# Narrower treatment of the entering steps in a windowed scan of test-time updates

## The chip, the cores and the metric

The kernel runs on one core of a Trainium2 chip. The metric is device time in microseconds (us), the median of several runs; before the change it is 901.47 us (three runs, 900.8 to 902.53). A profiled execution gives the trace that is read below. The engines are TensorE (PE for its matmuls, PEld for its weight loads), VectorE (DVE), ScalarE (ACT), GpSimd (POOL) and SyncE (SP), which here only issues transfers.

## The reference

Two layers follow one another on an input of 4 sequences, 1024 steps and 128 features. The second is a mixture of experts (8 experts, the best two of them for each token, and one shared expert); the change doesn't touch it. The first is a small two-layer network whose weights are trained while the sequence is read:

```python
def loss_fn(params, k_t, v_t):
    return jnp.mean((_mlp(params, k_t) - v_t) ** 2)

def step(params, kvt):
    k_t, v_t = kvt
    g = jax.grad(loss_fn)(params, k_t, v_t)
    new_params = tuple((p - LR * gp for p, gp in zip(params, g)))
    return (new_params, None)
params, _ = jax.lax.scan(step, (W1, b1, W2, b2), (k, v))
q = x @ W_Q
return _mlp(params, q)
```

Each of the 1024 steps sees 4 columns of k and v, one for each sequence, computes the gradient with the weights that all earlier steps have left, and takes one step of gradient descent. Only the weights after the last step are used further.

## The kernel before

The scan isn't run step by step. A window of `WIN = 32` steps, that is `R = 128` columns, slides over the sequence and advances by 6 and 7 steps in turn (`ADV = 7`). In each pass of the loop at line 555 (162 passes) all steps of the window are computed at once, from the weights as they stand before the window and from corrections for the steps of the window that lie earlier. The corrections use the previous pass's results, so that a step's values are refined about five times while it crosses the window. When steps leave at the front of the window, their update goes into the weights for good.

The main names are these:

- `z` (line 489): the hidden layer's input from the weights (`base`), to which line 569 adds the correction `dz` times `gm`. `gm` holds masked products of keys. They are computed in bands of 128 rows (`multiply` and `masked`, lines 382 to 403), written to DRAM (`g_dram`) and loaded again for each pass by `load_products` (line 319), six passes ahead, on SP's queue. Fourteen bands are computed before the scan, the others two at a time in the first passes.
- `at` and `th` (lines 598 and 600): Silu and tanh of `z`, on ACT; `mT` (line 607) combines them on DVE for the derivative.
- `y` (lines 582 and 613): the network's output; `nm` is the masked product of activations (`pg`, half 0, line 622), and `er` the errors of the previous pass.
- `et` (line 636): errors, `y` minus the wanted values; `vb` (`values`, line 494) are those values with the bias.
- `da` (lines 632 and 648): the gradient at the hidden layer; `hm` (line 579) is the masked product of errors (`pg`, half 1, line 659).
- `dz` (line 655): the gradient at the hidden layer's input.
- lines 678 and 679: POOL copies the leaving rows of `dz` and `er` (`dl`, `el`), with which `pu` and `pv` (lines 508 and 516) update the weights in the next pass.
- `add_changes` (line 533): POOL sums the squared changes of values between passes in `ch`, `sq`, `va` and `sums`. After the scan these sums decide whether the scan has converged. If it hasn't, a plain loop over all 1024 steps is run (line 730).

A window column exists only for the 32 steps inside. But the loop works ahead: `AHD = 7` steps next to enter, `AHD * B = 28` columns, are carried beside the 128 of the window, so the tiles are `C = R + 28 = 156` columns wide. For these, z, its correction, the activation, y with its correction, and the error are computed too. The products of activations and errors for the next pass (lines 622 and 659) then have columns for all steps of the next window.

The scan is under a manual schedule: each engine's instructions stand in the order in which the program writes them. On TensorE a pass has the order z from the correction, y from `nm`, `pu`, `pv`, y from the activations, the transposition of `at`, products of activations, transposition of `u`, transposition of `mT`, the two parts of `da`, transposition of `et`, products of errors, z of the next pass from the weights, transposition of `v`. Products of 32-bit numbers are two instructions each on TensorE, transpositions one. Each PSUM tile of the scan has one buffer.

Of the kernel before, what the change touches and what calls it, by code (L numbers as in the profile page):

```python
# [10 lines left out]
F32 = mybir.dt.float32  # L11
AF = mybir.ActivationFunctionType
ALU = mybir.AluOpType
# [4 lines left out]
P = 128  # L18
# [7 lines left out]
def kernel(  # L26
# [23 lines left out]
    nc = tc.nc  # L50
    B, S, D = x.shape
# [14 lines left out]
    AHD = ADV  # L66
    R = WIN * B
    Q = ADV * B
    C = R + AHD * B
# [9 lines left out]
    const = ctx.enter_context(tc.tile_pool(name="const", bufs=1))  # L79
# [49 lines left out]
    ident = const.tile([P, P], F32, name="ident")  # L129
# [13 lines left out]
    before = const.tile([P, WIN + ADV, B], F32, name="before")  # L143
# [24 lines left out]


    ad_bufs = [const.tile([P, D + 1], F32, name=f"ad{i}") for i in range(2)]  # L170
    nm_bufs = [const.tile([P, C], F32, name=f"nm{i}") for i in range(2)]
    dl_bufs = [const.tile([P, D], F32, name=f"dl{i}") for i in range(2)]
    el_bufs = [const.tile([P, D], F32, name=f"el{i}") for i in range(2)]

# [4 lines left out]
    def constants(n):  # L179

        if n == 0:


            nc.gpsimd.memset(before, -ALPHA)
            nc.gpsimd.affine_select(
                out=before, in_=before, compare_op=ALU.is_gt, fill=0.0, base=0,
                pattern=[[B, WIN + ADV], [0, B]], channel_multiplier=-1,
            )
        elif n == 1:
            for i in range(2):  # L190
                for t in (nm_bufs[i], dl_bufs[i], el_bufs[i]):
                    nc.gpsimd.memset(t, 0.0)
            nc.gpsimd.memset(sums, 0.0)
            nc.gpsimd.dma_start(eb1[:, 0:NE, :], e_b1)
            nc.gpsimd.dma_start(eb1[:, NE, :], s_b1)
        elif n == 2:
            nc.gpsimd.memset(eb1r, 0.0)
            nc.gpsimd.dma_start(wr_sb, w_router_t)
            nc.gpsimd.dma_start(sw1, s_w1t)
            nc.gpsimd.dma_start(sw2, s_w2t)  # L200
        elif n == 3:
            nc.gpsimd.memset(eb2, 0.0)
            for i in range(BLK):
                r = i * (P // BLK)
                nc.gpsimd.dma_start(eb2[r:r + NE, i, :], e_b2)
                nc.gpsimd.dma_start(eb2[r + NE:r + NX, i, :], s_b2.rearrange("(o d) -> o d", o=1))
        elif n == 4:
            sort_c["lane"] = iota("lane", [P], [[1, P]])
            sort_c["part"] = iota("part", [1], [[0, 1]], mult=1)
            sort_c["row1"] = iota(  # L210
                "row1", [TOP_K, NT], [[1, TOP_K], [TOP_K * P, NT]], base=1, mult=TOP_K
            )
            sort_c["edge"] = iota("edge", [NT], [[P, NT]])
            nc.gpsimd.memset(tri, 1.0)
            nc.gpsimd.affine_select(
                out=tri, in_=tri, compare_op=ALU.is_gt, fill=0.0, base=0, pattern=[[1, P]],
                channel_multiplier=-1,
            )
            for i in range(2):
                nc.gpsimd.memset(cum[i][:, 0:NT // 2, :], 0.0)  # L220
                nc.gpsimd.memset(ends[i][:, 0:NE // 2], 0.0)
# [41 lines left out]
    with tc.tile_pool(name="scanbig", bufs=1) as sbig, tc.tile_pool(  # L263
        name="kdram", bufs=1, space=DRAM
# [8 lines left out]
        g_dram = kdp.tile([NR, NR], F32, name="g_dram")  # L273
# [17 lines left out]
        PF = 6  # L291
# [27 lines left out]
        def load_products(i, queue):  # L319


            (op, pe), (o, e) = span(i - 1), span(i)
            el = min(e + AHD, S)
            gm = sp_.tile([P, C], F32, name="gm", bufs=PF + 1)
            queue.dma_start(
                gm[0:(pe - op) * B, 0:(el - o) * B], g_dram[op * B:pe * B, o * B:el * B]
            )
            return gm

# [45 lines left out]
            nc.sync.dma_start(tok(k_tok, j), kr)  # L375


        GW = Q + C + P
        gw_bufs = [sp_.tile([P, P + GW], F32, name=f"gw{i}", bufs=1) for i in range(4)]
        flat = before.rearrange("p s b -> p (s b)")  # L380

# [56 lines left out]
        for n in range(NBLK + 1):  # L438
# [19 lines left out]
            if n > B:  # L458
                for _ in range(4):
                    if todo[0] < early:  # L460
                        pg = bank("pgk", "k", [GW], 4)
# [6 lines left out]
            if n == B + 2:  # L468
                load_keys(0, nc.gpsimd)
                gms = {i: load_products(i, nc.gpsimd) for i in range(1, PF + 1)}  # L470
        load_keys(1, nc.gpsimd)
        front.close()
        before = flat
# [10 lines left out]
        with tc.tile_pool(name="s_ps", bufs=1, space=PSUM) as sps, tc.manual_schedule():  # L484
# [9 lines left out]
            def values(i, v):  # L494

                o, e = span(i)
                n = (min(e + AHD, S) - o) * B
                vb = sp_.tile([P, C], F32, name="vb")
                nc.scalar.activation(  # L499
                    vb[:, 0:n], vc[:, o * B:o * B + n], AF.Identity, bias=v[:, D:D + 1],  # L500
                    scale=-1.0,
                )
                return vb
# [44 lines left out]
            wa, wc, u, v = a_bufs[0], c_bufs[0], u_bufs[0], v_bufs[0]  # L548
# [3 lines left out]
            z = base(0, wa, True)  # L552
            vb = values(0, v)
            prev = pg = None
            for i in range(NI):
                o, e = span(i)
                op, pe = span(i - 1) if i else (0, 0)
                on, en = span(i + 1)
                ro, rn, q, qn = (pe - op) * B, (e - o) * B, (o - op) * B, (on - o) * B
                rc, nx = (min(e + AHD, S) - o) * B, (en - on) * B  # L560
# [1 line left out]

                y = sps.tile([P, C + P], F32, name="y")
                da = sps.tile([P, D], F32, name="da")
                if prev:
                    ae_p, ad_p, er_p, dz_p, q_p = prev
                    nc.tensor.matmul(  # L569
                        z[:, 0:rc], lhsT=dz_p[0:ro, :], rhs=gms.pop(i)[0:ro, 0:rc],  # L570
                        start=False, stop=True,
                    )
                    nm = nm_bufs[i % 2]
                    nc.vector.scalar_tensor_tensor(  # L574
                        nm[0:ro, 0:rn], pg[0:ro, 0, 0:rn], 1.0, before[0:ro, q:q + rn],
                        ALU.add, ALU.mult,
                    )
                    hm = sp_.tile([P, R], F32, name="hm")
                    nc.vector.tensor_tensor(
                        hm[0:ro, 0:rn], pg[0:ro, 1, 0:rn], before[0:ro, q:q + rn], ALU.mult  # L580
                    )
                    nc.tensor.matmul(  # L582
                        y[:, 0:rc], lhsT=er_p[0:ro, :], rhs=nm[0:ro, 0:rc],
                        start=True, stop=False,
                    )
                if i + PF < NI and i:
# [10 lines left out]
                at, et = ae[:, 0, :], ae[:, 1, :]  # L597
# [5 lines left out]
                if more is not None:  # L603
# [7 lines left out]


                nc.tensor.matmul(  # L613
                    y[:, 0:rc], lhsT=wc, rhs=at[:, 0:rc], start=not prev, stop=True
                )
                ta = z[:, C:C + P]
                nc.tensor.transpose(ta[0:rn, :], at[:, 0:rn], ident)  # L617
# [2 lines left out]
                if not last:  # L620
                    pg = sps.tile([P, 2, R], F32, name="pg")
                    nc.tensor.matmul(
                        pg[0:rn, 0, 0:nx], lhsT=at[:, 0:rn], rhs=at[:, qn:qn + nx],
                        start=True, stop=True,
# [6 lines left out]
                if prev:  # L631
                    nc.tensor.matmul(  # L632
                        da[0:rn, :], lhsT=hm[0:ro, 0:rn], rhs=ad_p[0:ro, 0:D],
                        start=True, stop=False,
                    )
                nc.vector.tensor_tensor(et[:, 0:rc], y[:, 0:rc], vb[:, 0:rc], ALU.add)
                v_new = update(v_bufs, v, pv) if q else v

                if not last:
                    vb = values(i + 1, v_new)  # L640
# [7 lines left out]
                nc.tensor.matmul(  # L648
                    da[0:rn, :], lhsT=et[:, 0:rn], rhs=v[:, 0:D], start=not prev, stop=True
                )  # L650
                nc.tensor.transpose(y[0:rn, C:C + P], et[:, 0:rn], ident)
                er = sp_.tile([P, D], F32, name="er")
                nc.scalar.copy(er[0:rn, :], y[0:rn, C:C + P])
                dz = sp_.tile([P, D], F32, name="dz")
                nc.vector.scalar_tensor_tensor(  # L655
                    dz[0:rn, :], da[0:rn, :], 0.5, dr[0:rn, :], ALU.mult, ALU.mult
                )
                if not last:
                    nc.tensor.matmul(
                        pg[0:rn, 1, 0:nx], lhsT=et[:, 0:rn], rhs=et[:, qn:qn + nx],  # L660
                        start=True, stop=True,
                    )
                    z = base(i + 1, wa, False)
                if q:
                    turn(pv, v_new)
                    wc = turned(c_bufs, wc, pv)
# [9 lines left out]
                if qn:  # L676
                    dl, el = dl_bufs[i % 2], el_bufs[i % 2]
# [7 lines left out]
                prev = (ae, ad, er, dz, q)  # L685
# [8 lines left out]
            wa, wc = turned(a_bufs, wa, pu), turned(c_bufs, wc, pv)  # L694
# [3 lines left out]
        with tc.tile_pool(name="f_sb", bufs=1) as fp, tc.tile_pool(  # L698
            name="f_ps", bufs=1, space=PSUM
# [30 lines left out]
        with tc.If(again > 0):  # L730
            load_params(wa, wc, u, v, nc.scalar)
            half_bias(u)
            with tc.tile_pool(name="o_sb", bufs=1) as op_, tc.tile_pool(
                name="o_ps", bufs=1, space=PSUM
            ) as ops:
                with tc.For_i(0, S, 1) as t:
# [22 lines left out]
                    for k, src in enumerate((kt, a1, d1, e1)):  # L759
# [19 lines left out]
                        start=True, stop=True,  # L779
# [13 lines left out]
    with ExitStack() as stage, tc.tile_pool(  # L793
        name="e_pa", bufs=3, space=PSUM
    ) as pa, tc.tile_pool(name="e_py", bufs=2, space=PSUM) as epy, tc.tile_pool(
        name="e_pt", bufs=2, space=PSUM
# [159 lines left out]
        at, d = 0, 1  # L956
        while d < NT:
# [3 lines left out]
            at, d = 1 - at, 2 * d  # L961
# [19 lines left out]
        at, d = 0, 1  # L981
        while d < NE:
# [4 lines left out]
            at, d = 1 - at, 2 * d  # L987
# [42 lines left out]
        for n, (k, g) in enumerate(groups):  # L1030
# [15 lines left out]
            for i in range(GC):  # L1046
                nc.tensor.matmul(  # L1047
                    inv, lhsT=sel[:, i, :], rhs=val[:, i, :],
                    start=(n == 0 and i == 0), stop=(n == len(groups) - 1 and i == GC - 1),
# [74 lines left out]
        for t in range(3):  # L1124
# [5 lines left out]
            rhs=code.rearrange("p t f -> p (t f)"), start=True, stop=True,  # L1130
# [4 lines left out]
        for h in range(2):  # L1135
            pg = bank(ept, "pg", "t", [NBLK // 2, P])
# [10 lines left out]
        prev = None  # L1147
        for t in range(NTL):
# [10 lines left out]
            prev = (t, hs, ws.pop(t)[1])  # L1159
# [77 lines left out]
```

## Time and profile before

| | |
|---|---|
| median of three runs | 901.47 us |
| profiled execution | 901.75 us |
| its span, first to last instruction | 899.9 us |
| mean granted TensorE clock | 0.974 of full speed |
| PE busy / PEld busy | 811.0 us (90%) / 741.6 us (82%) |
| DVE busy / ACT busy / POOL busy | 525.2 / 503.8 / 554.2 us |
| scan with its first passes | about 65 to 575 us |
| y from nm (line 582), 128x156 | mean 330 ns of one instruction, 196 between 200 and 500 us |
| y from the activations (line 613), 128x156 | mean 311 ns |
| z from gm (line 569), 128x156 | mean 298 ns |
| products of errors (line 659), 128x128 | mean 275 ns |
| values (line 499), 128x156 | mean 424 ns |
| errors (line 636), 128x156 | mean 321 ns |

[...] What one costs in a stream is the distance from its start to the start of the next matmul, which the view in order of time shows. In that view "x2" means two instructions merged in one row, with the time from the start of the first to the end of the second. Times in the trace are counted from the start of the span.

### The profile page before, as it was taken

What the parts mean: (1) busy time and instruction counts of PE and PEld (TensorE: products, weight loads), DVE (VectorE), ACT (ScalarE), POOL (GpSimd) and SP (SyncE); (2) the same over time, 40 slices, a digit from 0 to 9 for tenths busy, and PEclk for the clock granted to TensorE, in tenths of its full rate; (3) what the DMA queues carried; (4) which work ended last, traced back from release to release, by engine and by line L of the source; (5) the groups of instructions that cost most, each with busy time, mean ns of one, the idle gap of its engine ahead of it and who ended that gap; (6) DMA issues with size and microseconds to landing.
All of it is one profiled execution on the core that took longest, in us unless ns stands there. A gap on an engine that the chain in (4) does not pass through costs nothing. (4 is left out here: it accounts for less than half of the span.)

```text
span 899.9 us, 21051 instructions
## 1 busy us (share of the span) xinstructions
PE 811.0 (90%) x6164; PEld 741.6 (82%) x6164; DVE 525.2 (58%) x1904; ACT 503.8 (56%) x1571; POOL 554.2 (62%) x1513
## 2 busy tenths in 40 slices
PE   4789999999999999999999999788999999999830
PEld 3456899999999999999999999555479999899730
DVE  5634577677677677767767776475973232223227
ACT  2564566666666666666666666355623444444432
POOL 6630577777777777777777777521015777777730
PEclk9999999999999999999999999998999999999975
DMA  5273311121111111121111110002115777778755
GB/s 129 73 233 119 97 31 27 26 49 27 28 29 39 34 30 26 29 46 27 29 28 26 30 27 7 2 25 71 58 42 163 243 254 237 240 241 259 248 172 167
DMA packets 77892, 82.48 MB, mean 92 GB/s; under 512 B 9907, under 2 KB 57023, under 8 KB 77777
## 3 DMA queue, kind: packets, MB, share of 16 engines
q1 hardware_dynamic: 68880, 68.16, 25.2%
q0 software_dynamic: 5632, 10.07, 4.1%
q10 hardware_dynamic: 3264, 2.89, 1.0%
q8 instruction: 51, 0.84, 0.4%
q14 instruction: 65, 0.52, 0.2%
HBM read 64.03 MB, written 17.97 MB: 91 GB/s over the span
## 5 line engine op out<-in xcount | busy, mean ns | idle before, releaser
L1097 ACT ACTIVATE hs<-ph,b1t 128x128 f32<-128x128 f32 x284 | 81.1, 369 | 109.2 <-PE ph L1093 100.8
L678 POOL COPY dl<-dz 24x128 f32<-24x128 f32 (+2 forms) x158 | 44.5, 281 | 148.9 <-DVE dz L655 148.9
L1066 POOL DMA_INDIRECT xg<-h_tab,toks_i x71 | 72.9, 1026 | 73.8 <-DVE toks_i L1062 52.4
L521 DVE SCALAR_TENSOR_TENSOR u<-pu,u 128x130 f32<-128x130 f32 x158 | 46.4, 294 | 115.3 <-PE pu L508 115.3
L546 POOL TENSOR_TENSOR sums<-sums,sq 128x48 f32<-128x48 f32 (+2 forms) x315 | 93.8, 317 | 0.0
L1110 POOL DMA_INDIRECT y_tab<-yg,rows_i x71 | 72.5, 1021 | 29.7 <-issue 13.1
L619 ACT COPY ad<-z 128x128 f32<-128x128 f32 (+3 forms) x162 | 43.0, 265 | 73.0 <-PE z L617 73.0
L582 PE MATMUL y<-nm,er 128*128 128x156 f32 (+4 forms) x322 | 79.3, 328 | 3.1 <-DVE nm L574 2.7
L1093 PE MATMUL ph<-xT,w1t 128*128 128x128 f32 x568 | 75.3, 276 | 0.7 <-DVE xT L1086 0.7
L1105 PE MATMUL py<-w2t,hs 128*128 128x128 f32 x568 | 74.9, 275 | 0.0
L613 PE MATMUL y<-ae,c 128*128 128x156 f32 (+3 forms) x324 | 73.2, 307 | 0.0
L530 ACT COPY c<-pv 128x128 f32<-128x128 f32 x158 | 42.0, 266 | 52.5 <-PE pv L526 49.6
L569 PE MATMUL z<-gm,dz 128*128 128x156 f32 (+4 forms) x322 | 69.7, 298 | 0.2
L1093 PEld LDWEIGHTS ph<-xT,w1t 128*128 128x128 f32 x568 | 68.9, 191 | 0.9 <-DVE xT L1086 0.9
L489 PE MATMUL z<-kT,a 128*128 128x156 f32 (+3 forms) x324 | 69.6, 296 | 0.0
L1105 PEld LDWEIGHTS py<-w2t,hs 128*128 128x128 f32 x568 | 69.0, 192 | 0.0
L499 ACT ACTIVATE vb<-vT,v 128x156 f32<-128x156 f32 (+3 forms) x162 | 68.2, 421 | 1.4 <-DVE dr L642 1.0
L539 POOL TENSOR_TENSOR sq<-ch 128x104 f32<-128x104 f32 (+1 forms) x158 | 56.9, 360 | 12.4
L598 ACT ACTIVATE ae<-z,u 128x156 f32<-128x156 f32 (+3 forms) x162 | 62.8, 387 | 2.8 <-PE z L569 0.9
L648 PE MATMUL da<-v,ae 128*128 128x128 f32 (+3 forms) x324 | 62.9, 276 | 0.1
L632 PE MATMUL da<-ad,hm 128*128 128x128 f32 (+3 forms) x322 | 62.4, 275 | 0.0
L538 POOL TENSOR_TENSOR ch<-ae 128x104 f32<-128x104 f32 (+1 forms) x158 | 62.4, 395 | 0.0
(245 smaller groups left out, 2390.9 us busy)
## 6 DMA issues: line engine op xcount, KB each, us to landing
w1t<-in_e_w1t_dram SPq DMA_DIRECT2D x71, 256.0 KB
w2t<-in_e_w2t_dram SPq DMA_DIRECT2D x71, 256.0 KB
gm<-g_dram SPq DMA_DIRECT2D x150, 78.0 KB
g_dram<-gw SPq DMA_DIRECT2D x29, 220.0 KB
x_sb<-in_x_dram SPq DMA_DIRECT2D x8, 256.0 KB
k_dram<-kr SPq DMA_DIRECT2D x8, 256.0 KB
h_tab<-hr SPq DMA_DIRECT2D x8, 256.0 KB
hs_all<-y_tab ACTq DMA_DIRECT2D x4, 512.0 KB
```

What stands on the lines that cost most here:

```text
L489: nc.tensor.matmul(z[:, 0:n], lhsT=wa, rhs=kc[:, o * B:o * B + n], start=True, stop=alone)
L499: nc.scalar.activation(vb[:, 0:n], vc[:, o * B:o * B + n], AF.Identity, bias=v[:, D:D + 1], scale=-1.0,)
L546: nc.gpsimd.tensor_tensor(t, t, x_[:, :, c0:c1], ALU.add)
L569: nc.tensor.matmul(z[:, 0:rc], lhsT=dz_p[0:ro, :], rhs=gms.pop(i)[0:ro, 0:rc], start=False, stop=True,)
L582: nc.tensor.matmul(y[:, 0:rc], lhsT=er_p[0:ro, :], rhs=nm[0:ro, 0:rc], start=True, stop=False,)
L613: nc.tensor.matmul(y[:, 0:rc], lhsT=wc, rhs=at[:, 0:rc], start=not prev, stop=True)
L648: nc.tensor.matmul(da[0:rn, :], lhsT=et[:, 0:rn], rhs=v[:, 0:D], start=not prev, stop=True)
L1066: nc.gpsimd.indirect_dma_start(out=xg_bufs[t % 6][:], out_offset=None, in_=h_tab[:, :], in_offset=bass.IndirectOffsetOnAxis(ap=toks_i[:, t ...
L1093: nc.tensor.matmul(ph[:, f, :], lhsT=w1t[:, ts(f, P)], rhs=xT, start=True, stop=True)
L1097: nc.scalar.activation(hs[:, f, :], ph[:, f, :], AF.Gelu_apprx_tanh, bias=b1t[:, t, f:f + 1])
L1105: nc.tensor.matmul(py, lhsT=hs[:, f, :], rhs=w2t[:, f, :], start=(f == 0), stop=(f == NFC - 1))
L1110: w = nc.gpsimd.indirect_dma_start(out=y_tab[:, :], out_offset=bass.IndirectOffsetOnAxis(ap=rows_i[:, t:t + 1], axis=0), in_=yg[:], in_off ...
```

## The change

For the steps next to enter, only z from the weights (without its correction) and the activation from it are still computed. The correction of z, both parts of y, the values, the errors and the products of errors have columns for the window alone. The steps that have just entered therefore have no products of errors from the previous pass: these columns of `hm` are zero. `hm` moves to two fixed buffers that are zeroed once, and only its first `ro - q` columns are written in each pass; where a pass writes fewer columns than the pass before it in the same buffer, a memset clears the rest. `nm` moves to the rotating pool in exchange. The key products lose the 28 columns in their bands (`GW`) and in `gm`.

```diff
-    nm_bufs = [const.tile([P, C], F32, name=f"nm{i}") for i in range(2)]
+    hm_bufs = [const.tile([P, R], F32, name=f"hm{i}") for i in range(2)]
...
-            el = min(e + AHD, S)
-            gm = sp_.tile([P, C], F32, name="gm", bufs=PF + 1)
+            gm = sp_.tile([P, R], F32, name="gm", bufs=PF + 1)
             queue.dma_start(
-                gm[0:(pe - op) * B, 0:(el - o) * B], g_dram[op * B:pe * B, o * B:el * B]
+                gm[0:(pe - op) * B, 0:(e - o) * B], g_dram[op * B:pe * B, o * B:e * B]
             )
...
-        GW = Q + C + P
+        GW = Q + R + P
...
-                n = (min(e + AHD, S) - o) * B
-                vb = sp_.tile([P, C], F32, name="vb")
+                n = (e - o) * B
+                vb = sp_.tile([P, R], F32, name="vb")
...
-                y = sps.tile([P, C + P], F32, name="y")
+                y = sps.tile([P, R + P], F32, name="y")
...
-                        z[:, 0:rc], lhsT=dz_p[0:ro, :], rhs=gms.pop(i)[0:ro, 0:rc],
+                        z[:, 0:rn], lhsT=dz_p[0:ro, :], rhs=gms.pop(i)[0:ro, 0:rn],
                         start=False, stop=True,
                     )
-                    nm = nm_bufs[i % 2]
+                    nm = sp_.tile([P, R], F32, name="nm")
...
-                    hm = sp_.tile([P, R], F32, name="hm")
+                    hm = hm_bufs[i % 2]
                     nc.vector.tensor_tensor(
-                        hm[0:ro, 0:rn], pg[0:ro, 1, 0:rn], before[0:ro, q:q + rn], ALU.mult
+                        hm[0:ro, 0:ro - q], pg[0:ro, 1, 0:ro - q], before[0:ro, q:ro],
+                        ALU.mult,
                     )
+                    if hm_cols[i % 2] > ro - q:
+                        nc.vector.memset(hm[:, ro - q:hm_cols[i % 2]], 0.0)
+                    hm_cols[i % 2] = ro - q
                     nc.tensor.matmul(
-                        y[:, 0:rc], lhsT=er_p[0:ro, :], rhs=nm[0:ro, 0:rc],
+                        y[:, 0:rn], lhsT=er_p[0:ro, :], rhs=nm[0:ro, 0:rn],
...
-                    y[:, 0:rc], lhsT=wc, rhs=at[:, 0:rc], start=not prev, stop=True
+                    y[:, 0:rn], lhsT=wc, rhs=at[:, 0:rn], start=not prev, stop=True
...
-                nc.vector.tensor_tensor(et[:, 0:rc], y[:, 0:rc], vb[:, 0:rc], ALU.add)
+                nc.vector.tensor_tensor(et[:, 0:rn], y[:, 0:rn], vb[:, 0:rn], ALU.add)
...
-                        pg[0:rn, 1, 0:nx], lhsT=et[:, 0:rn], rhs=et[:, qn:qn + nx],
+                        pg[0:rn, 1, 0:rn - qn], lhsT=et[:, 0:rn], rhs=et[:, qn:rn],
```

Here `o` and `e` are the first step and the end of the window, `rn` its columns, `rc` those with the steps ahead, `ro` the columns of the previous window, and `q` the columns by which the window has advanced.

More of the change, by code (lines that the diff above doesn't have):

```diff
@@ L190, in constants @@
             for i in range(2):
-                for t in (nm_bufs[i], dl_bufs[i], el_bufs[i]):
+                for t in (hm_bufs[i], dl_bufs[i], el_bufs[i]):
                     nc.gpsimd.memset(t, 0.0)
@@ L554 @@
             prev = pg = None
+            hm_cols = [0, 0]
             for i in range(NI):
@@ L650 @@
                 )
-                nc.tensor.transpose(y[0:rn, C:C + P], et[:, 0:rn], ident)
+                nc.tensor.transpose(y[0:rn, R:R + P], et[:, 0:rn], ident)
                 er = sp_.tile([P, D], F32, name="er")
-                nc.scalar.copy(er[0:rn, :], y[0:rn, C:C + P])
+                nc.scalar.copy(er[0:rn, :], y[0:rn, R:R + P])
                 dz = sp_.tile([P, D], F32, name="dz")
```

## The prediction

> **What bounds the kernel now.** I read the views from coarse to fine. The busy tenths by slice put TensorE at 9 in every slice from about 70 us to 560 us: that stretch is the scan, the only part that the diff touches apart from one band width before it. The busy time by stretch shows what fills it:
>
> ```profile
> 200.00:250.00 50.00, 50.00 (x412) 49.38 (x410) 34.92 (x132) 33.84 (x116) 37.57 (x132) 1.00 0.11 28
> ```
>
> The columns after the length are PE, PEld, DVE, ACT and POOL busy, then the granted clock (1.00), the DMA share and GB/s. PE and PEld are full, but matmul ends are modelled, so "full" alone doesn't say that a shorter matmul makes a shorter pass. For that I took the scan's period apart in the order of time, from the start of one `da<-v,ae` (D) to the next. A steady pass (columns: start us, us, engine, line, operation):
>
> ```profile
> 404.54 0.39 PE L648 MATMUL da<-v,ae 128*128 128x128 f32 x2
> ...
> 406.33 0.36 POOL L539 TENSOR_TENSOR sq<-ch 128x104 f32<-128x104 f32 x1
> 406.44 0.30 PEld L613 LDWEIGHTS y<-ae,c 128*128 128x128 f32 x2
> ...
> 406.70 0.37 DVE L607 SCALAR_TENSOR_TENSOR mT<-ae,th 128x128 f32<-128x128 f32 x1
> 406.81 0.27 PE L617 MATMUL z<-ident,ae 128*128 128x128 f32 x1
> ...
> 407.58 0.39 PE L648 MATMUL da<-v,ae 128*128 128x128 f32 x2
> ```
>
> The period is 407.58 - 404.54 = 3.04 us. There are 147 of them: the group of mT between 106 and 556 us has 147 entries, and 147 x 3.05 = 448 us.
>
> The most useful rows stand at the end of the scan. Where the sequence runs out, the extra columns vanish by themselves, and one pass of the old kernel already runs z, y and the values 128 wide:
>
> ```profile
> 557.52 0.39 PE L648 MATMUL da<-v,ae 128*128 128x128 f32 x2
> ...
> 559.32 0.36 POOL L539 TENSOR_TENSOR sq<-ch 128x104 f32<-128x104 f32 x1
> 559.36 0.30 PEld L613 LDWEIGHTS y<-ae,c 128*128 128x128 f32 x2
> ...
> 559.65 0.41 DVE L607 SCALAR_TENSOR_TENSOR mT<-ae,th 128x128 f32<-128x128 f32 x1
> 559.68 0.27 PE L617 MATMUL z<-ident,ae 128*128 128x128 f32 x1
> ...
> 560.51 0.39 PE L648 MATMUL da<-v,ae 128*128 128x128 f32 x2
> ```
>
> Its period is 2.99 us. The reader is to see three things. The transposition at line 617 comes at D + 2.27 in the steady pass and at D + 2.16 here, so TensorE did gain 0.11 us. The square on POOL ends at the same place in both (D + 2.15 and D + 2.16). And mT, the next DVE operation, runs from there: 406.70 is 0.01 behind the end of sq at 406.69, and although the 128-wide pass records mT from 559.65, it takes 0.41 instead of 0.37, and ends at D + 2.54 against D + 2.53. So half of TensorE's gain was lost again, waiting for mT.
>
> **The change part by part.** Widths become 128 instead of 156 in three matmuls of two passes each (z from gm, y from nm, y from wc), in the values (ACT), in the errors (DVE), and in the gm transfer; 100 or 104 instead of 128 in the key products of the errors (line 659) and hm; 284 instead of 312 in the band products (line 384). Nothing is moved: no instruction changes its place on an engine, and no wait is added in the scan. The base matmul (line 489) and Silu stay 156 wide.
>
> *TensorE.* In the steady pass a 156-wide matmul starts its successor 0.27 us later (405.47 to 405.74, z from gm), a 128-wide one 0.22 (404.54 to 404.76). So z from gm, y from nm and y from wc should give 3 x 0.05 = 0.15. The last products with 104 columns gave 0.20 against 0.22 (560.84 to 561.04), 0.02 more: 0.17 in all if TensorE alone set the pace. [...] PEld is busy 49.38 of 50 us. [...]
>
> *What the gain runs into.* I follow the chain in the new kernel from D, with durations from the two passes. dz starts at D + 0.48 and ends at 0.77, unchanged. The load for z from gm follows 0.05 behind dz (405.31 to 405.36; 558.30 to 558.35), so the 0.02 of the products brings nothing. Its second pass starts two loads later (0.215), ends 0.275 after that, and Silu follows 0.10 later: D + 1.41 (it was 1.46; 1.42 at the end of the scan). Silu takes 0.39, and the load for y from wc comes 0.05 behind: 1.85. The transposition follows 0.32 later instead of 0.37: 2.17. By TensorE's order alone the next da would stand 0.77 later, as in the steady pass (406.81 to 407.58): D + 2.94, a gain of 0.10.
>
> But tm needs mT. mT reads two SBUF tensors while POOL reads SBUF. [...] sq hangs on dz through POOL's queue (dl, el, ch, sq), and none of these change; so sq ends at D + 2.15, mT at 2.53. From the end of mT to da the 128-wide pass took 0.45 (560.06 to 560.51), as did a pass near the start (89.23 to 89.68). New period: 2.98, a gain of **0.06**. [...] I take 0.06, since the end of the scan is the nearest row there is.
>
> 147 x 0.06 = **8.8 us**.
>
> *The first passes* also multiply a band each time. Sixteen of these are 312 wide inside the scan, 0.53 us apart in the stretch at 92.31 to 92.84, and lose 28 columns: 28/312 x 0.53 = 0.05 each, 0.8 us, on the path since masking, nm and u wait for them (0.41 us idle before y from nm there). The narrower y in the last four of these passes gives 2 x 0.05 x 4 = 0.4. Together **1.2 us**. Before the scan 14 bands lose 0.05 each, but only some lie on TensorE's path between other stages: 0 to 0.7, I take **0.5**.
>
> *Costed at nothing.* The values (424 ns at 156, 0.40 at 128) end well before y needs them. hm is behind nm, and ahead of u, which waits 69.8 us over 98 passes (0.71 each) for its matmul. The errors shrink from 0.32 to 0.28, but wait for mT. gm shrinks from 78 to 64 KB on SP's queue, asked for six passes ahead, and no engine waits for it. Three memsets of hm in the last passes (24 and 52 columns), at most 0.16 us each by the smallest mT, also lie in front of u. If the cover were gone they would cost 0.5 us. [...]
>
> **Sum**: 8.8 + 1.2 + 0.5 = 10.5 us. Against the profiled execution, 901.75 us (span 899.9), 891.2. That run lies 0.28 above the median shown, 901.47; so 891.0.
>
> **The rivals.** [...] (2) *TensorE alone*: 0.17 x 147 + 1.7 = 26.7, **875 us**. For it, two full rows; against it, the loads behind dz, Silu and mT all come within 0.06 of the ends that they wait for. (3) *Weight loads or the POOL chain hold everything*: gain under 0.02 a pass, 898 to **901 us**. The tail's 2.99 speaks against it, but that is one pass. [...] (5) *The change isn't what it says*: the scan tests its own convergence and, failing, repeats everything in 1024 single steps, milliseconds. Entering steps start from poorer values, so I worked the recurrence through in single precision on the reference's inputs: the squared change of the last pass over that of the one before is 0.0053 and 0.0026 (0.0042 and 0.0037 before the change) against a limit of 0.25, and the extrapolated rest 1.2e-9 and 1.5e-9 against 5.4e-8 and 9.3e-8. It isn't taken.
>
> **How the numbers follow.** The forecast 0.60 (887 to 894 by itself: 0.04 to 0.085 a pass), rival 1 0.16, rival 2 0.05, rival 3 0.09, rival 4 0.09, rival 5 0.01. The time is that of the forecast, 891.0. The range 883.5 to 897.5 takes in the forecast, most of rival 1 and the better third of rival 3. About 0.2% (1.8 us) is what the measurement can tell from no change: faster 0.60 + 0.16 + 0.05 + 0.04 = 0.85, same 0.05 from rival 3, slower 0.10.
>
> **What would show it.** Right: periods of 2.98; y from nm and y from wc starting their successors 0.05 to 0.07 sooner; mT behind sq as before and ending at D + 2.53; the transposition at line 617 (old numbering) near D + 2.17 and a gap of some 0.04 us at tm. [...]

## The result and the profile after

The changed kernel takes **889.07 us** (median of four runs, 888.6 to 894.81) against 901.67 (four runs, 900.8 to 902.53): ratio 0.9875, 95% interval 0.9834 to 0.9916. The forecast was 891.0. The profiled execution takes 888.6 us with a span of 886.8, 13.1 less than before (899.9), at nearly the same mean clock (0.972; 0.974 before).

I cut both spans at the same instructions (first `pu`, steady `da`, the first matmul of `pqw` behind the scan, the first `inv` of the mixture of experts):

| stretch, us | before | after | gained | forecast |
|---|---|---|---|---|
| up to the scan's first `pu<-ident,a` | 65.14 | 64.23 | 0.91 | 0.5 |
| first passes | 42.41 | 41.21 | 1.20 | 1.2 |
| 148 steady passes | 452.96 | 440.05 | 12.91 | 8.8 (147 passes) |
| end of the scan, up to `pqw` | 20.06 | 20.08 | 0 | 0 |
| `pqw` to `inv` (router, shared expert) | 68.17 | 70.36 | -2.19 | 0 |
| `inv` to the end | 251.16 | 250.87 | 0.29 | 0 |

The median period is 2.96, 3.05 before. The busy time by stretch of the changed kernel (PE, PEld, DVE, ACT, POOL, clock, DMA share, GB/s):

```profile
200.00:250.00 50.00, 50.00 (x425) 49.75 (x424) 33.64 (x136) 33.61 (x119) 39.90 (x137) 1.00 0.10 24
```

The weight loads are as full as before (49.75 us of 50; 49.38 before), yet the same 50 us hold 425 rows of matmuls instead of 412: a full PEld was no sign that nothing could be gained. A steady pass of the changed kernel in order of time:

```profile
396.92 0.39 PE L652 MATMUL da<-v,ae 128*128 128x128 f32 x2
...
397.75 0.30 PEld L569 LDWEIGHTS z<-gm,dz 128*128 128x128 f32 x2
...
398.34 0.39 ACT L602 ACTIVATE ae<-z,u 128x156 f32<-128x156 f32 x1
...
398.63 0.36 ACT L604 ACTIVATE th<-z,u 128x128 f32<-128x128 f32 x1
398.72 0.36 POOL L538 TENSOR_TENSOR sq<-ch 128x104 f32<-128x104 f32 x1
398.78 0.30 PEld L617 LDWEIGHTS y<-ae,c 128*128 128x128 f32 x2
398.82 0.29 DVE L520 SCALAR_TENSOR_TENSOR u<-pu,u 128x130 f32<-128x130 f32 x1 [0.69 <-PE pu L507]
...
399.03 0.28 DVE L611 SCALAR_TENSOR_TENSOR mT<-ae,th 128x128 f32<-128x128 f32 x1
399.03 0.41 POOL L541 TENSOR_TENSOR va<-ae 128x48 f32<-128x48 f32 x1
...
399.11 0.27 PE L621 MATMUL z<-ident,ae 128*128 128x128 f32 x1
...
399.88 0.39 PE L652 MATMUL da<-v,ae 128*128 128x128 f32 x2
```

With D = 396.92: Silu at D + 1.42 (1.46 before), the load for y from wc at 1.86 (1.90), the transposition at 2.19 (2.27), the next `da` 0.77 behind it, at 2.96. Of the steady pass before (D = 404.54), beside the rows already shown, these matter:

```profile
406.00 0.39 ACT L598 ACTIVATE ae<-z,u 128x156 f32<-128x156 f32 x1
...
406.50 0.29 DVE L521 SCALAR_TENSOR_TENSOR u<-pu,u 128x130 f32<-128x130 f32 x1 [0.71 <-PE pu L508]
...
406.65 0.28 POOL L542 TENSOR_TENSOR va<-ae 128x56 f32<-128x56 f32 x1
```

The surprise is mT. It takes 0.28 us instead of 0.37, and now it is POOL's `va` that takes 0.41. The groups between 200 and 500 us (the last columns are total us and mean ns of one, then idle time ahead of them) say so of every pass; first before, then after:

```profile
L607 DVE SCALAR_TENSOR_TENSOR mT<-ae,th 128x128 f32<-128x128 f32 x98 | 36.0, 367 | 0.2
...
L542 POOL TENSOR_TENSOR va<-ae 128x56 f32<-128x56 f32 x49 | 13.8, 281 | 0.0
L542 POOL TENSOR_TENSOR va<-ae 128x48 f32<-128x48 f32 x49 | 13.1, 268 | 0.0
```

```profile
L611 DVE SCALAR_TENSOR_TENSOR mT<-ae,th 128x128 f32<-128x128 f32 x100 | 28.7, 287 | 0.4
L541 POOL TENSOR_TENSOR va<-ae 128x56 f32<-128x56 f32 x51 | 21.3, 417 | 0.0
L541 POOL TENSOR_TENSOR va<-ae 128x48 f32<-128x48 f32 x50 | 19.8, 396 | 0.0
```

The two run side by side in both kernels, and the loser of the pair has changed. The forecast's period of 2.98 had mT losing.

### The profile page after: what moved, and what is told of

It reads as the page before. It is cut to its first block, busy times and chain, and to the rows that moved or that the text cites. A ratio compares the mean times of both kernels' runs of the same rounds, so it can differ in the third digit from the quotient of the medians.

```text
span 886.8 us, 21054 instructions
## 1 busy us (share of the span) xinstructions
PE 797.3 (90%) x6164; PEld 732.3 (83%) x6164; DVE 502.0 (57%) x1907; ACT 491.0 (55%) x1571; POOL 564.8 (64%) x1513
## 5 line engine op out<-in xcount | busy, mean ns | idle before, releaser
L545 POOL TENSOR_TENSOR sums<-sums,sq 128x48 f32<-128x48 f32 (+2 forms) x315 | 86.0, 291 | 0.0
L586 PE MATMUL y<-nm,er 128*128 128x128 f32 (+3 forms) x322 | 73.4, 310 | 3.4 <-DVE nm L574 2.7
L488 PE MATMUL z<-kT,a 128*128 128x156 f32 (+3 forms) x324 | 72.9, 307 | 0.0
L617 PE MATMUL y<-ae,c 128*128 128x128 f32 (+3 forms) x324 | 69.0, 294 | 0.0
L498 ACT ACTIVATE vb<-vT,v 128x128 f32<-128x128 f32 (+3 forms) x162 | 65.0, 401 | 1.2 <-DVE dr L646 0.9
L569 PE MATMUL z<-gm,dz 128*128 128x128 f32 (+3 forms) x322 | 62.8, 277 | 0.2
L541 POOL TENSOR_TENSOR va<-ae 128x48 f32<-128x48 f32 (+2 forms) x158 | 62.7, 397 | 0.0
```

The costliest lines, as they stand in the source:

```text
L488: nc.tensor.matmul(z[:, 0:n], lhsT=wa, rhs=kc[:, o * B:o * B + n], start=True, stop=alone)
L498: nc.scalar.activation(vb[:, 0:n], vc[:, o * B:o * B + n], AF.Identity, bias=v[:, D:D + 1], scale=-1.0,)
L545: nc.gpsimd.tensor_tensor(t, t, x_[:, :, c0:c1], ALU.add)
L569: nc.tensor.matmul(z[:, 0:rn], lhsT=dz_p[0:ro, :], rhs=gms.pop(i)[0:ro, 0:rn], start=False, stop=True,)
L586: nc.tensor.matmul(y[:, 0:rn], lhsT=er_p[0:ro, :], rhs=nm[0:ro, 0:rn], start=True, stop=False,)
L617: nc.tensor.matmul(y[:, 0:rn], lhsT=wc, rhs=at[:, 0:rn], start=not prev, stop=True)
```

## The experiments

The kernels ran in three groups, on chips with different levels (before takes 908.04 on the first, 943.37 on the second, 943.43 on the third), so totals are compared within a group and periods across groups. The higher level of the last two groups lies behind `inv`, where no edit reaches: that stretch takes 289 to 292 us in their profiles and 251 to 254 in the others. "Period" is the median distance of two `da<-v,ae` in the steady scan.

### One half of the change at a time

The kernel before, with the narrow z correction alone:

```diff
-            el = min(e + AHD, S)
-            gm = sp_.tile([P, C], F32, name="gm", bufs=PF + 1)
+            gm = sp_.tile([P, R], F32, name="gm", bufs=PF + 1)
...
-        GW = Q + C + P
+        GW = Q + R + P
...
-                        z[:, 0:rc], lhsT=dz_p[0:ro, :], rhs=gms.pop(i)[0:ro, 0:rc],
+                        z[:, 0:rn], lhsT=dz_p[0:ro, :], rhs=gms.pop(i)[0:ro, 0:rn],
```

In this expectation and some later ones, "port theory" stands for a supposition of mine, that mT waits for the end of POOL's sq. No run shows a port.

> The kernel before, with the correction of z (and its key products, bands and gm) narrowed to 128 columns, and all else as before. Chain theory (load of y from the activations behind Silu, order on TensorE behind it): Silu starts at D + 1.42 instead of 1.46, but y from the activations is held by TensorE's own order behind the late, wide y from nm; period 3.02 (gain 0.02 to 0.03), some 897 us. TensorE's sum alone: gain 0.05, period 3.00, some 893 us. Port theory (mT behind sq): mT ends at D + 2.53 with 0.37 us, period 3.0 at the least.

Measured: period 3.02, 905.73 us (before in this group: 908.04; one run each). A pass in order of time:

```profile
401.09 0.39 PE L647 MATMUL da<-v,ae 128*128 128x128 f32 x2
...
402.51 0.39 ACT L597 ACTIVATE ae<-z,u 128x156 f32<-128x156 f32 x1
...
402.74 0.30 PEld L515 LDWEIGHTS pv<-ad,el 128*128 128x128 f32 x2
...
402.96 0.30 PEld L612 LDWEIGHTS y<-ae,c 128*128 128x128 f32 x2
```

The changed kernel with these same lines put back to the wide form, so that only the correction of z keeps the entering columns:

```diff
-        GW = Q + R + P
+        GW = Q + C + P
...
-                        z[:, 0:rn], lhsT=dz_p[0:ro, :], rhs=gms.pop(i)[0:ro, 0:rn],
+                        z[:, 0:rc], lhsT=dz_p[0:ro, :], rhs=gms.pop(i)[0:ro, 0:rc],
```

> The kernel after, with the correction of z (bands and gm too) 156 wide again; y, values, errors and products of errors stay narrow. Chain theory: Silu back at D + 1.46, load of y from the activations at 1.90, transposition 0.32 later, period 2.99 to 3.00, gain 0.05 over before, some 893 to 895 us. TensorE's sum alone: gain 0.12, period 2.93. Port theory: mT from D + 2.16 and 0.37 us as before, period 2.99.

Measured: period 3.00, 897.04 us. To three digits the periods are 3.048 before, 3.021 with the narrow correction of z alone, 3.004 with the rest alone and 2.959 with both. The halves are worth 0.027 and 0.044, the whole 0.089, so 0.018 a pass comes only from having both. The expectation for the first half names the reason, and the lines above agree: Silu starts at D + 1.42, as in the changed kernel, but y from `nm` is still wide and late, and the load for y from the activations stands at D + 1.87 instead of 1.86, without a gap behind the two loads for `pv` (0.11 us each). So only part of what Silu gained got through. In the changed kernel all of it does: making the correction of z wide again costs 0.045 there.

Both halves work on one chain, as the forecast had it. The narrow y, values and errors of the second half weren't taken apart any further. The totals of the two runs (2.3 and 11.0 us below before) are single runs and too coarse for these differences.

### POOL's sums taken away

In the changed kernel and in the one before, the sums of squared changes are left out (so nothing is gathered for the convergence test); POOL then has only its two copies in the pass:

```diff
-                if prev:
+                if False:
```

> The kernel after without the sums of squared changes on POOL (the scan's test for convergence then sees zeros and passes). Chain theory: mT isn't on the path, period 2.96 as after, time 888 to 889 us. Port theory: mT, freed of POOL, ends earlier, and the period falls towards TensorE's sum, 2.90 or less, 879 us or less.

> The kernel before without the sums of squared changes on POOL (the test for convergence sees zeros). Chain theory: mT takes 0.28 instead of 0.37 us and ends earlier, and the period stays 3.04 to 3.05, time 900 to 902 us. Port theory: period under 3.00, 894 us or less.

Measured: 2.91 and 885.16 us from the changed kernel, 3.02 and 898.44 from the one before. Neither theory hit: the chain gave no gain (2.96; 3.04 to 3.05), the port theory a larger one (at most 2.90; under 3.00). Both kernels gain, although mT is lengthened beside va in one of them only (0.37 us before, 0.28 in the changed kernel). Since mT already took 0.28 in the changed kernel, a delay of mT by POOL can't be what the missing sums gave back. Nor does mT wait for POOL before it starts. A pass of the changed kernel without the sums:

```profile
402.81 0.39 PE L652 MATMUL da<-v,ae 128*128 128x128 f32 x2
...
404.71 0.29 DVE L520 SCALAR_TENSOR_TENSOR u<-pu,u 128x130 f32<-128x130 f32 x1 [0.70 <-PE pu L507]
...
404.92 0.28 DVE L611 SCALAR_TENSOR_TENSOR mT<-ae,th 128x128 f32<-128x128 f32 x1
...
405.73 0.39 PE L652 MATMUL da<-v,ae 128*128 128x128 f32 x2
```

There is no sq here, and mT starts at D + 2.11, where it starts with the sums. (In the kernel before it is D + 2.17 with the sums and without.) Something else came with POOL's work. It shows at Silu: with the sums it starts 0.23 us behind the start of the copy of `c` ahead of it on ACT (398.11 to 398.34), without them 0.16 to 0.17 (401.09 to 401.25 and 404.00 to 404.17).

### A fifth buffer for the tile that Silu writes

The view of one line's instructions counts, for Silu's line in the changed kernel, an entry of ACT's queue beside the activations (minimum, median and maximum ns, first and last start):

```profile
L602 ACTq EVENT_SEMAPHORE  x156: 17/17/17, 64.7 to 555.9; - x156
```

Silu writes `ae`, which has four buffers, and POOL reads the tiles of two passes for `ch`. So Silu waits for two engines, TensorE (z) and POOL (the buffer), and one of the waits is an instruction of its own. In the records of the trace this instruction starts 0.063 us ahead of Silu (median of the passes between 200 and 500 us). Taking POOL's readers away removes it (one is left in the kernel without sums). A fifth buffer should remove it too, with all of POOL's work kept:

```diff
-                ae = sp_.tile([P, 2, C], F32, name="ae", bufs=4)
+                ae = sp_.tile([P, 2, C], F32, name="ae", bufs=5)
```

> The kernel after with five buffers instead of four for the tile that holds activations and errors. Silu then waits for TensorE alone, not for TensorE and POOL. Second-semaphore theory: Silu starts 0.06 us earlier behind the correction of z (D + 1.36 instead of 1.42), as in the runs without the sums, the load of y from the activations follows at D + 1.81, and the period is 2.91; 147 x 0.05 = 7 us less than after, 881 to 883 us, though POOL does all its sums. POOL-work theory (it is the sums themselves, through the SBUF port or POOL's queue, that cost 0.05): the period stays at 2.96 and the time at 889 us.

Measured: period **2.91**, as without the sums. The same view, with five buffers:

```profile
L602 ACTq EVENT_SEMAPHORE  x1: 17/17/17, 64.6 to 64.6; - x1
```

And a pass of this kernel in order of time:

```profile
401.21 0.39 PE L652 MATMUL da<-v,ae 128*128 128x128 f32 x2
...
402.40 0.27 ACT L529 COPY c<-pv 128x128 f32<-128x128 f32 x1 [0.33 <-PE pv L525]
...
402.57 0.39 ACT L602 ACTIVATE ae<-z,u 128x156 f32<-128x156 f32 x1
...
403.02 0.30 PEld L617 LDWEIGHTS y<-ae,c 128*128 128x128 f32 x2
...
404.12 0.39 PE L652 MATMUL da<-v,ae 128*128 128x128 f32 x2
```

Silu at D + 1.36 instead of 1.42, the load at 1.81 instead of 1.86, `da` at 2.91 instead of 2.96: the 0.06 at Silu arrives at the end almost whole.

The fifth buffer removes a second wait on DVE too, since the errors are written into the same tile. In the changed kernel the view of their line has

```profile
L640 DVEq EVENT_SEMAPHORE  x155: 21/21/21, 96.5 to 556.9; - x155
```

and with five buffers no such entry; the errors start 0.12 us sooner behind D. It isn't this that shortened the pass: `da` stands 0.77 behind the transposition in both kernels, the length of TensorE's own order between the two, and the transposition doesn't need the errors.

The same edit in the kernel before:

> The kernel before with five buffers, so that Silu waits for TensorE alone, with all sums on POOL. Second-semaphore theory: Silu at D + 1.40 as in the kernel before without the sums, period 3.02. POOL-work theory: 3.05.

Measured: period 3.02 with all of POOL's sums in place, equal to the kernel before without them, Silu at D + 1.40 (403.72 from 402.32), 940.16 us beside 943.43. This separates the second wait from POOL's work: the work stayed, mT still took 0.37, and the gain came all the same. It is smaller here (0.03) because the load for y from the activations stops at D + 1.87, as with the narrow correction of z alone: Silu is 0.06 sooner, and TensorE's own order allows only 0.03 of it.

### The order of mT and va

What let mT win in the changed kernel? The products of errors are narrower and end earlier (0.37 us with 104 columns at 397.26; 0.39 with 128 at 557.86 in the trace before). I put their full width back and nothing else:

```diff
-                        hm[0:ro, 0:ro - q], pg[0:ro, 1, 0:ro - q], before[0:ro, q:ro],
+                        hm[0:ro, 0:ro - q], pg[0:ro, 1, q:ro], before[0:ro, q:ro],
...
-                        pg[0:rn, 1, 0:rn - qn], lhsT=et[:, 0:rn], rhs=et[:, qn:rn],
+                        pg[0:rn, 1, 0:rn], lhsT=et[:, 0:rn], rhs=et[:, 0:rn],
```

> The kernel after with the products of errors 128 columns wide again (the same values, in other columns). Chain theory: what the 100 and 104 columns save at the products is given back at the next matmul, z from the weights, whose weight load comes too early to be used; z from gm stays behind dz; period 2.96, time 888 to 890 us. TensorE's sum: 0.02 more a pass, period 2.98, 892 us.

Measured: period 2.98, 930.8 us. A pass in order of time:

```profile
400.84 0.39 PE L652 MATMUL da<-v,ae 128*128 128x128 f32 x2
...
402.96 0.28 POOL L541 TENSOR_TENSOR va<-ae 128x56 f32<-128x56 f32 x1
...
402.97 0.41 DVE L611 SCALAR_TENSOR_TENSOR mT<-ae,th 128x128 f32<-128x128 f32 x1
...
403.82 0.39 PE L652 MATMUL da<-v,ae 128*128 128x128 f32 x2
```

mT comes 0.01 behind va, takes 0.41, ends at 403.38, and `da` follows 0.44 later, at D + 2.98. This is the forecast's pass, number for number. Of the two expectations, TensorE's sum had the period right, but not the way: the matmuls' own 0.02 stays hidden, as the other expectation said (the transposition stands at D + 2.19 with either width). (The total of one run can't show 3 us; the periods can.) The 0.02 of the products reaches mT by a way that the forecast didn't follow: `nm` reads the same PSUM tile `pg`, so it starts at D + 0.74 in the changed kernel and at 0.76 here; y from nm's load follows at 1.15 and 1.17, `pu` at 1.47 and 1.49, u at 1.90 and 1.92, mT at 2.11 and 2.13. POOL's va is at 2.11 and 2.12 whichever. In the 13 or 14 passes of each kernel between 380 and 420 us:

| kernel | mT's start against va's | mT, us | va, us |
|---|---|---|---|
| before | 0.05 to 0.06 behind | 0.36 to 0.38 | 0.27 to 0.28 |
| full-width products | 0.01 to 0.02 behind | 0.40 to 0.41 | 0.27 to 0.28 |
| changed | 0.00 to 0.02 ahead | 0.28 to 0.29 | 0.40 to 0.42 |

In all three, the one that starts first takes its 0.27 to 0.29 us, and the other pays. mT itself starts 0.21 behind the start of u in all three, and in both kernels without sums. Only in the kernel with the wide correction of z does it start later (0.25), 0.03 behind the end of `th`.

The second test puts another POOL instruction beside mT, by moving va ahead of ch (so that sq takes its place):

```diff
+                nc.gpsimd.tensor_tensor(va[:, :, 0:n], cur[:, :, 0:n], cur[:, :, 0:n], ALU.mult)
                 nc.gpsimd.tensor_tensor(ch[:, :, 0:n + m], cur, old, ALU.subtract)
...
-                nc.gpsimd.tensor_tensor(va[:, :, 0:n], cur[:, :, 0:n], cur[:, :, 0:n], ALU.mult)
```

> The kernel after with the squares of the values put ahead of the changes on POOL, so that sq runs when mT is ready. Full exclusion on the port (mT waits until sq has ended and then takes 0.28): mT ends at D + 2.7, da stands at 3.17, 30 us more, some 919 us. Partial sharing (the loser pays about 0.09 us): mT takes 0.37, ends at D + 2.48, and the period stays 2.96, time 888 to 890 us.

Measured: period 2.98, 933.53 us, which neither theory had:

```profile
402.83 0.36 POOL L539 TENSOR_TENSOR sq<-ch 128x104 f32<-128x104 f32 x1
402.92 0.42 DVE L611 SCALAR_TENSOR_TENSOR mT<-ae,th 128x128 f32<-128x128 f32 x1
...
403.78 0.39 PE L652 MATMUL da<-v,ae 128*128 128x128 f32 x2
```

If mT had to wait for the whole of sq's record, it would have ended 0.28 behind the end of sq, at 403.47. It ended at 403.34, and `da` stood 0.44 behind that. But the loser paid 0.14 and not the 0.09 of the second theory. How long the first holds up the second can be read from the steady passes of several kernels (medians, us; "added" is beside 0.281 for mT without POOL's sums, and beside 0.267 for va in the kernel before):

| first of the two, its record | kernel | second starts behind it | added to the second | sum |
|---|---|---|---|---|
| va, 48 columns, 0.267 | before | 0.053 | 0.079 | 0.132 |
| va, 48 columns, 0.266 | wide correction of z | 0.031 | 0.101 | 0.132 |
| va, 48 columns, 0.265 | full-width products | 0.017 | 0.116 | 0.132 |
| va, 56 columns, 0.281 | before | 0.052 | 0.094 | 0.146 |
| sq, 104 columns, 0.359 | va ahead of ch | 0.074 | 0.152 | 0.226 |
| mT, 128 columns, 0.284 | changed (va second) | 0.004 | 0.137 | 0.141 |

For va of 48 columns the sum is 0.132 whenever the second starts; it is larger for a wider first (0.146 with 56 columns, 0.226 with 104), and the first pays nothing. This speaks against sharing in part and fits a wait of the second, but only until a point that lies 0.13 to 0.14 us before the recorded end of the first (0.267 less 0.132, 0.359 less 0.226). What the first does in the rest of its record, and what the two contend for, isn't shown.

### Nothing ahead at all

The changed kernel with no entering columns even in z from the weights, Silu and the products of activations. The limit of the convergence test is widened by a factor of 4, so that the scan isn't repeated in single steps:

```diff
-    AHD = ADV
+    AHD = 0
...
-    TOL = 2.0 ** -15
+    TOL = 2.0 ** -13
...
-                        pg[0:rn, 0, 0:nx], lhsT=at[:, 0:rn], rhs=at[:, qn:qn + nx],
+                        pg[0:rn, 0, 0:rn - qn], lhsT=at[:, 0:rn], rhs=at[:, qn:rn],
```

> The kernel after without any columns for the entering steps: z from the weights, Silu and the products of activations have the window's columns alone (28 fewer each), and the limit of the scan's convergence test is 16 times as wide in the square sums. Chain theory: z from gm is held by dz, Silu starts at D + 1.41 but takes 0.365 instead of 0.39, period 2.90, some 879 to 881 us. If the chain behind dz and Silu doesn't hold: TensorE's sum, 2.96 less 0.09, period 2.87, some 876 us.

Measured: period 2.91, 925.66 us, close to the chain theory (Silu at D + 1.41, 0.37 us long). Another 0.05 by the same means, while a fifth buffer gets the same 0.05 and gives up nothing of the computation.

### The two kernels once more, side by side

> The kernel after, unchanged, beside the run with five buffers on the same chip. Period 2.96 whatever the chip, 12 to 13 us less than before.

> The kernel after with five buffers, beside the kernel after on the same chip. Second-semaphore theory: period 2.91, 7 us less than after, 19 to 20 us less than before.

Measured on the third chip: the changed kernel 930.5 us (926.33 to 936.88), ratio to before 0.9864, interval 0.9809 to 0.992, period 2.96; with five buffers **922.99 us** (920.88 to 924.95), ratio 0.9785, interval 0.9758 to 0.9812, period 2.91. On the second chip five buffers gave 924.37 and 0.9802 (0.9764 to 0.984). The medians put the fifth buffer's worth at some 7.5 us on top of the change. The steady stretch of the two profiles became 6.3 us shorter (440.05 and 433.75), near 148 x 0.046 = 6.8 (the periods to three digits are 2.959 and 2.913; some ten passes, of up to 3.3 us in both kernels, gain less). This version beats both kernels.

### The 2.2 us lost behind the scan

No instruction between `pqw` and `inv` differs, yet this stretch became longer. The clock accounts for it. Here is the busy time by stretches of 5 us, of which only those behind `pqw` with a low clock are given (third column from the end). First before:

```profile
580.50:585.50 5.00, 4.53 (x8) 1.90 (x8) 0.16 (x1) 1.59 (x3) 1.95 (x8) 0.66 0.01 2
620.50:625.50 5.00, 4.04 (x21) 3.52 (x20) 0.85 (x2) 1.59 (x3) 0.00 (x0) 0.62 0.18 56
625.50:630.50 5.00, 4.90 (x8) 1.80 (x7) 2.78 (x7) 4.94 (x7) 0.00 (x0) 0.70 0.17 54
```

Then after:

```profile
565.50:570.50 5.00, 4.53 (x7) 2.15 (x8) 0.17 (x1) 1.00 (x3) 1.94 (x8) 0.53 0.01 2
...
600.50:605.50 5.00, 3.22 (x23) 2.72 (x23) 4.06 (x17) 2.04 (x3) 1.27 (x2) 0.88 0.24 74
605.50:610.50 5.00, 4.13 (x20) 3.73 (x20) 0.00 (x0) 1.36 (x2) 0.00 (x0) 0.50 0.27 87
610.50:615.50 5.00, 5.00 (x14) 2.97 (x14) 1.61 (x4) 3.09 (x4) 0.00 (x0) 0.59 0.17 54
```

Time lost to the clock, (1 - clock) x 5 summed over the stretch, is 5.1 us before (0.34 + 0.38 + 0.30 = 1.02) and 7.5 after (0.47 + 0.12 + 0.50 + 0.41 = 1.50): 2.4 more, for 2.2 us more of time. The thirteen profiles of this study hold to it: the three with 5.1 to 5.3 us lost (before, the one with the wide z correction, the one with nothing ahead) take 68.2 to 68.3 us there, the ten with 7.2 to 8.5 take 70.1 to 71.0. In the clock records the first spell lasts 3.4 or 6.8 us, the second 6.8 or 10.2. Kernels with the change and kernels without it stand in both groups, so the loss isn't simply the change's. But the changed kernel and the one with five buffers were each traced twice and were in the slower group both times, and no kernel was traced in both groups. Whether the level belongs to the execution or to the timing of the kernel stays open; what sets the length of the spells wasn't tried.

## Why the prediction was right

**The bound: right.** One chain through dz, Silu, y, the transposition and `da` sets the period. Both halves of the change shortened it, and so did the narrow products. The weight loads, full as they are (49.75 of 50 us), weren't a limit. Narrower matmuls did start their successors sooner: z from gm starts its successor 0.24 later instead of 0.27, and the transposition stands 0.33 behind y's load instead of 0.37.

**Links of the chain.** dz (D + 0.48) and the load for z from gm (0.83) stayed. Silu was put at 1.41 and stands at 1.42, the load for y from wc at 1.85 and 1.86, the transposition at 2.17 and 2.19, `da` 0.77 behind it. By TensorE's order the forecast had 2.94; the chip has 2.96.

**The mis-sized term: the wait for mT.** The forecast added 0.04 because mT was to end at D + 2.53; it ends at D + 2.39 and costs nothing. The forecast therefore came out at 2.98 in place of 2.96, and the steady gain at 0.06 a pass. No run shows the term in this sum, a wait of mT for the end of sq; the runs show mT starting 0.21 behind u, and 0.074 behind the start of sq where that stands beside it (va ahead of ch). Two steps behind the term failed:

- "So the 0.02 of the products brings nothing." It brings nothing to z, as said. It does bring 0.02 to `nm`, and by way of `pu` and u to mT, which was enough to turn the order of mT and va. With full-width products the forecast's 2.98 is the measured period. The pass at the end of the scan, from which the number was taken, had the narrow z, y and values, but the products of errors at its beginning (at 557.86 in the trace before) were still 128 wide.
- "mT, the next DVE operation, runs from there", that is, from the end of sq. mT follows u by 0.21 in every kernel but the one with the wide correction of z, with POOL's sums and without, and with sq ahead of it or beside it. That sq ended at the same moment was a coincidence; what delays mT, or is delayed by it, is the instruction that POOL runs beside it (va, or sq in the kernel with va ahead of ch).

The delay itself didn't go away with the change: in the changed kernel it adds 0.13 to 0.14 us in each pass (va takes 0.396 and 0.417 us instead of 0.268 and 0.281). It just falls on va, for which nobody waits. In the kernel with full-width products it falls on mT (0.116) and costs 0.02 a pass.

**The forecast's own signs.** Two of them speak against the way in which it reached its number: mT ended at D + 2.39 and not at 2.53, and `tm` starts without a gap, 0.11 behind the matmul ahead of it (399.44 to 399.55). The two parts of y start their successors 0.04 sooner (0.29 instead of 0.33 for y from `nm`; for y from wc the 0.37 and 0.33 given above), a little less than the 0.05 to 0.07 asked for.

**A cost that was counted without being seen.** "Silu follows 0.10 later" was read from the trace and was right, but 0.06 of it was the second wait. Being the same in both kernels it didn't hurt the forecast, and removing it was worth 6 to 7.5 us more.

**The sum.** The steady passes gave 12.9 instead of 8.8: 0.087 each (452.96 less 440.05, over 148) instead of 0.06, just outside the 0.04 to 0.085 that the forecast allowed. The first passes gave 1.2 as forecast. The stretch before the scan gave 0.9 instead of 0.5, beyond the bounds of 0 to 0.7; but a second profile of the changed kernel, on another chip, takes 65.55 us there where this one takes 64.23, so the 0.9 can't be put down to the bands. Against it stand 2.2 us lost to the clock behind the scan, where the forecast had nothing. 15.0 gained in the first three stretches, less 1.9 in the last two, is 13.1; the forecast had 10.5. That the total came within 2 us is in good part luck: 4.1 us too little forecast for the steady passes, and 2.2 lost where nothing was forecast. The convergence fallback (rival 5) wasn't taken: the stretch from the end of the steady passes to `pqw` is as long as before (20.08 and 20.06 us).

## What to carry to other kernels

When a row of the old trace stands in for the new kernel, list what that row still lacks of the change, and follow the missing piece down every reader of what it produces, not only the one on the critical path. Where instructions of two engines lengthen one another, as mT and va did here, ask which starts first: a shift of 0.02 us decided who paid 0.13. And look in the queue rows for semaphore instructions ahead of a critical operation: one more buffer turned two waits into one and gave 6 to 7.5 us on top of the whole edit's 12.6.

## What the runs showed of the hardware

- **The second wait cost more than its record.** The extra semaphore instruction on ACT is recorded with 17 ns, yet it delays Silu by 0.06 us and the pass by 0.05 (2.96 to 2.91) in the changed kernel; in the one before the pass loses 0.03 (3.05 to 3.02). Four more instructions of ACT in each pass (line 529 twice, 498 and 657) have such an entry; what these cost wasn't tried. By the order of the program POOL had read that buffer for the last time more than a pass earlier.
- **mT on DVE and the POOL instruction beside it delayed one another, for less than the recorded time.** The one that starts second takes 0.40 to 0.42 us instead of 0.27 to 0.28 when it starts within 0.02 us of the first; if it had to wait for all of the first, it would take about 0.55 (an estimate, the two usual times added up). The added time fits a wait that ends 0.132 us behind the start of a va of 48 columns (recorded 0.267), 0.146 behind one of 56 (0.281) and 0.226 behind a sq of 104 (0.359), so 0.13 to 0.14 us ahead of the first one's recorded end. The one that starts first keeps its usual time.
- **The clock fell at the seam behind the scan.** In the stretch ahead of `pqw` TensorE is busy for 1.0 us of 5 (both kernels), and around its end the granted clock fell to 0.5, and again 40 us later. By stretches of 1 us the first spell has three at 0.50 before (581 to 584) and six after (564 to 570). How long the spells last goes with 2 to 3 us in a stage that no edit touched, about a fifth of the gain measured here.
